# Multi-query attention with residual on one Trainium2 core: two instruction paddings in the front in place of nine, and the last four residuals loaded earlier in the final list

## The chip, the cores and the metric

The kernel runs on one core of a Trainium2 chip. The metric is the device time of one launch in microseconds (us); a lower one is better. TensorE is called PE (its weight loads PEld), VectorE DVE, ScalarE ACT, GpSimd POOL and SyncE SP. Every DMA that this text speaks of is issued by SP, in the order of the program.

## The reference

Sixty-four batches of 128 tokens with 512 features go through a layer norm, multi-query attention with 16 heads of width 64 (one key and value head for all), an output projection, a second layer norm, and a residual sum. All is float32.

```
xn  = layernorm(x, g_in)                              # 64 x 128 x 512
q   = (xn @ Wq).reshape(b, n, 16, 64) * 64 ** -0.5
kv  = xn @ Wkv                                        # one head: k, v
k, v = null_kv and kv, concatenated along the tokens  # 129 keys
sim = einsum('bhid,bjd->bhij', q, k) + bias           # bias per head, null column
sim = where(causal or mask, -max, sim)
out = einsum('bhij,bjd->bhid', softmax(sim), v) @ Wo
y   = x + layernorm(out, g_out)
```

## The kernel before

**Tiling.** Tokens come in groups of four batches (512 tokens, 16 groups). Two batches are one round of the main loop, `cycle(c)` for c from 1 to 29. A round does several things for different batches side by side: it loads and norms the tokens of a later group, makes the queries of the next group (`q_one`, seven products in the manner of Strassen's scheme per pair of feature tiles), the exponentials and sums of its own two batches (`exps`, `rinv`, `scale`), the output projection of the two batches before (`out_one`), the output norm and the store of the two before those, and, in `region(c)`, the scores of the next two batches and the product of the present ones with the values. Queries of group 0 are made in a plain way by `q_half(c, h)`: four matrix products of 128 x 128 by 128 x 256 into one PSUM tile, 8 pairs of a weight load and a matmul in the instruction stream, and then a copy by ACT. The PSUM tile of `q_half(c, 1)` has one of two buffers, X for even c and Y for odd c, so it waits for the copy of `q_half(c - 2, 1)`.

**Order.** Nothing reorders the program (`tc.manual_schedule()`): each engine works through its instructions in the order in which the Python code makes them. The code has a front written out by hand (L1079 to L1229: group 0, first scores, first queries of group 1), the loop (L1230), and a final list written out by hand (L1234 to L1375) for the last six batches, in which the output norm is cut into `pair_stats`, `pair_pow`, `pair_center`, `pair_scale` and `store`.

**Paddings.** `nc.tensor.addr_align(256, offset=k)` fills PE's instruction stream with NOPs until the next instruction stands k slots behind a multiple of 256 slots. A weight load, a matmul, a NOP and a wait on a semaphore of its own are one slot each. There are nine such calls in the front (L1151, L1156, L1161, L1167, L1177, L1188, L1200, L1213, L1218) and one in each round of the loop (L1058), with the offset 223, or 183 in the last round, ahead of `region(c)`.

**Residuals and stores.** `load_res(b)` (L131) takes a buffer of 128 x 512 and loads the input x[b] again; `pair_scale(b)` (L822) adds it to the normed output on DVE; `store(b)` (L835) writes the result. Residuals take the two `res` buffers, those of the last four batches the three `x` buffers, which held input tokens in the loop. The outputs y of a round are in three buffers called `y`; those of the last six batches are in one tile of their own, `y_end`. A load into a buffer waits for the last reader of what the buffer held, and SP, which issues it, waits with all that stands behind. In the final list the order on SP is: load_res(B-6), load_res(B-5), store(B-8), load_res(B-2), load_res(B-4), load_res(B-3), load_res(B-1), store(B-7), store(B-6), store(B-5), store(B-3), store(B-4), store(B-2), store(B-1), with B = 64. Ahead of it stand the stores and the two residual loads of round 29.

## Time and profile before

| | us |
|---|---|
| median of 3 runs | 1051.45 (1051.0 to 1051.99) |
| the profiled execution, its own time | 1052.77 |
| its span, from the first to the last instruction | 1051.0 |
| PE busy | 1028.5 |
| DVE busy | 772.0 |
| POOL busy | 710.1 |
| ACT busy | 665.5 |
| mean granted TensorE clock | 0.994 |

The span is what the profile's views divide; the time of the execution has 1.77 us more, which lie before and after the instructions. The three runs were taken without the profiler. A row of a timeline gives start, length, engine, line, operation, tiles and count, and in brackets the idle time ahead of it and what ended it. "issue" in that place means that the profile shows no wait. A row of the windows gives, for one stretch, its length, the busy time of PE, PEld, DVE, ACT and POOL, the granted clock of TensorE, the busy share of the 16 DMA engines and the GB/s that they moved.

### The profile page before, as it was taken

How to read it: one execution, taken by the hardware profiler on the slowest of the kernel's cores; microseconds unless marked ns; L12 is line 12 of the kernel's file. 1: busy time of each engine (PE TensorE's matmuls, PEld its weight loads, DVE VectorE, ACT ScalarE, POOL GpSimd, SP SyncE). 2: the span in 40 equal slices, each digit the busy share in tenths (PEclk: the TensorE clock that was granted, in tenths of full speed). 3: DMA queues.
4: the chain of work that ended last, by engine and by line, in shares of the span. 5: the costliest groups of instructions: out<-in, count | busy, mean ns of one | idle time of the engine just before them, and what ended most of it. 6: DMA issues, size and time to landing. Idle time of an engine off the chain costs nothing.

```text
span 1051.0 us, 31264 instructions
## 1 busy us (share of the span) xinstructions
PE 1028.5 (98%) x11856; PEld 899.5 (86%) x11856; DVE 772.0 (73%) x1664; ACT 665.5 (63%) x2799; POOL 710.1 (68%) x530
## 2 busy tenths in 40 slices
PE   9699999999999999999999999999999999999996
PEld 8588888888888888888888888888888888888875
DVE  7467777776868767877776867767877776766698
ACT  3267766667766667766667766667765667755581
POOL 3478767577575776767577575776767577676774
PEclk9899999999999999999999999999999999999999
DMA  6615052341514315052341514316052341502103
GB/s 213 153 50 140 22 159 77 110 131 47 157 50 133 113 62 171 25 160 77 111 131 46 158 48 133 113 66 170 26 152 80 109 131 47 159 7 82 42 7 135
DMA packets 68690, 105.12 MB, mean 100 GB/s; under 512 B 8640, under 2 KB 32832, under 8 KB 66752
## 3 DMA queue, kind: packets, MB, share of 16 engines
q1 hardware_dynamic: 67440, 102.08, 32.0%
q8 instruction: 97, 1.59, 0.7%
q10 hardware_dynamic: 1104, 1.05, 0.3%
q14 instruction: 49, 0.40, 0.1%
HBM read 67.45 MB, written 35.65 MB: 98 GB/s over the span
## 4 chain that ended last, share of the span: by engine, by line
PE 77%; DVE 8%; ACT 6%; POOL 4%; DMA 2%; issue 2%; SPq 0%; POOLq 0%; ACTq 0%; DVEq 0%
PE pa L493 16%; PE pyX L755 15%; PE pyY L755 8%; PE pc L493 8%; PE ps L548 8%; PE pkv L355 5%; PE pyw L755 4%; PE pw L493 4%; PE poX L665 4%; ACT s L596 3%; PE pq L442 3%; DMA xT<-xd 2%; PE pos L665 2%; POOL s L617 1%; DVE sb L632 1%
## 5 line engine op out<-in xcount | busy, mean ns | idle before, releaser
L596 ACT ACTIVATE s<-s,nmax 128x65 f32<-128x65 f32 (+1 forms) x1024 | 377.3, 392 | 0.0
L532 POOL TENSOR_TENSOR s<-biasp,mneg 128x1552 f32<-128x1552 f32 x64 | 206.2, 3223 | 70.7 <-DVE sb L632 58.9
L617 POOL TENSOR_TENSOR s<-s,rinv 128x1024 f32<-128x1024 f32 (+1 forms) x128 | 190.0, 1485 | 56.9 <-DVE rinv L613 56.9
L596 ACT ACTIVATION_READ_ACCUMULATOR s<-s,nmax 128x1 f32 x1024 | 220.2, 215 | 0.0
L632 DVE STREAM_TRANSPOSE sb<-s 128x1536 f32<-128x1536 f32 x64 | 113.5, 1773 | 42.4 <-POOL s L617 42.2
L582 DVE TENSOR_TENSOR s<-ps,s 128x256 f32<-128x256 f32 (+2 forms) x224 | 120.1, 607 | 18.0 <-PE ps L548 15.7
L493 PE MATMUL pa<-xS,wq 128*128 128x256 f32 x480 | 123.4, 379 | 0.5 <-ACT ku L504 0.5
L755 PE MATMUL pyX<-wo,oT 128*128 128x256 f32 x512 | 121.6, 380 | 0.2 <-POOL oT L738 0.2
L738 POOL TENSOR_TENSOR yS<-oT 128x512 f32<-128x512 f32 x32 | 40.7, 1273 | 118.3 <-ACT oT L705 114.2
L705 ACT ACTIVATE oT<-poX,nv 128x256 f32<-128x256 f32 x59 | 28.0, 474 | 143.8 <-PE poX L665 74.4
L587 DVE TENSOR_REDUCE nmax<-s 128x8 f32<-128x520 f32 (+1 forms) x128 | 116.6, 951 | 0.0
L755 PE MATMUL pyX<-wT,oT 128*128 128x256 f32 x488 | 115.4, 379 | 0.3 <-POOL oT L738 0.3
L755 PEld LDWEIGHTS pyX<-wo,oT 128*128 128x128 f32 x512 | 96.8, 190 | 15.3 <-issue 1.3
L755 PEld LDWEIGHTS pyX<-wT,oT 128*128 128x128 f32 x488 | 92.6, 190 | 13.3 <-POOL oT L738 0.7
L493 PEld LDWEIGHTS pa<-xS,wq 128*128 128x128 f32 x480 | 88.9, 190 | 11.7 <-ACT ku L504 0.9
L548 PEld LDWEIGHTS ps<-kT,qT 64*64 64x64 f32 x4096 | 85.6, 134 | 11.3 <-issue 11.1
L548 PE MATMUL ps<-kT,qT 64*64 64x128 f32 (+1 forms) x4096 | 93.7, 245 | 0.3 <-issue 0.3
L514 DVE TENSOR_TENSOR qT<-pc,ku 128x256 f32<-128x256 f32 x120 | 50.4, 420 | 58.4 <-ACT ku L504 43.1
L511 ACT COPY qT<-pa 128x256 f32<-128x256 f32 x60 | 23.0, 383 | 101.9 <-PE pa L493 101.9
L665 PE MATMUL pos<-sb,vr 32*64 32x128 f32 (+1 forms) x1792 | 81.0, 321 | 0.0
L285 POOL TENSOR_TENSOR rstd<-rstd,nhalf 128x1 f32<-128x1 f32 x64 | 35.6, 558 | 66.0 <-DVE rstd L284 66.0
L665 PE MATMUL poY<-sb,vr 32*64 32x128 f32 x720 | 74.4, 347 | 0.0
(113 smaller groups left out, 2306.1 us busy)
## 6 DMA issues: line engine op xcount, KB each, us to landing
x<-in_x_dram SPq DMA_DIRECT2D x64, 256.0 KB, 5.1
res<-in_x_dram SPq DMA_DIRECT2D x64, 256.0 KB, 3.0
out_dram<-y SPq DMA_DIRECT2D x58, 256.0 KB, 2.0
xd<-xb SPq DMA_DIRECT2D x14, 1024.0 KB
xT<-xd SPq DMA_DIRECT2D x56, 256.0 KB, 6.2
vr<-vd SPq DMA_DIRECT2D x64, 128.0 KB, 8.6
kT<-kd SPq DMA_DIRECT2D x64, 64.0 KB, 9.6
kd<-kb SPq DMA_DIRECT2D x16, 128.0 KB
```

Of the source, the lines that this page charges most:

```text
L355: nc.tensor.matmul(pkv, xT[g][:, t, kc, :], wkv[:, kc, :], start=(kc == 0), stop=(kc == KC - 1),)
L493: nc.tensor.matmul(prod[tag], w[:, kc, f * P : (f + 1) * P], t[:, :, kc, :], start=(start and kc == 0), stop=(kc == HK - 1), skip_group_ch ...
L514: nc.vector.tensor_tensor(o, p, k, ALU.add)
L532: nc.gpsimd.tensor_tensor(S[b], biasp, mneg[:, t].unsqueeze(1).broadcast_to([P, R8, ROW]), ALU.add,)
L548: nc.tensor.matmul(to[r][i * DH : (i + 1) * DH, f, :], qT[g][rows, f, t, NQ - 1 - i if hf else i], kT[g][rows, 0 : NQ if hf else NQ // 2, ...
L582: nc.vector.tensor_tensor(sv, ps, sv, ALU.add)
L587: nc.vector.tensor_reduce(nmax[b][:, hf], S[b][:, :, WITH_NULL[hf]], AX.X, ALU.max, negate=True)
L596: nc.scalar.activation(row, row, AF.Exp, bias=nmax[b][:, hf, k : k + 1], accum_out=rsum[b][:, hf, k : k + 1],)
L617: nc.gpsimd.tensor_tensor(sv, sv, rinvs.pop((b, hf)).unsqueeze(2).broadcast_to([P, R8, sv.shape[2]]), ALU.mult,)
L632: nc.vector.transpose(sb.rearrange("p j e q -> p e j q"), S[b][:, :, 1 : ROW - 1].rearrange("p e (j k) -> p e j k", k=Q),)
L665: nc.tensor.matmul(po[s][rows, half], vr[g][quad(s), j, t, :], sb[quad(s), slots, r * NF : (r + 1) * NF, :], start=start, stop=True, skip_ ...
L755: nc.tensor.matmul(prod[key], h[:, c, :], w[:, c, :], start=(start and c == 0), stop=(c == HC - 1), skip_group_check=not start,)
```

## The change

Seven of the nine paddings in the front go; the other two, at L1161 and L1188, get other offsets (244 for 149, 86 for 24). The paddings of the loop stay. In the final list, the residual loads of the last four batches move to its head, in the order B-4, B-3, B-2, B-1; the one of batch B-1 takes a `y` buffer, since three `x` buffers hold the others. No other instruction moves; each store of the final list now has no residual load between it and the store before, save load_res(B-6) and load_res(B-5), which stay.

```
     def load_res(b):
-        pool, tag = (xp, "x") if b >= B - 4 else (rp, "res")
-        res[b] = pool.tile([P, DIM], FP, tag=tag, name=f"res_{b}")
+        if b == B - 1:
+            res[b] = hp.tile([P, DIM], FP, tag="y", name=f"res_{b}", bufs=3)
+        else:
+            pool, tag = (xp, "x") if b >= B - 4 else (rp, "res")
+            res[b] = pool.tile([P, DIM], FP, tag=tag, name=f"res_{b}")
         nc.sync.dma_start(out=res[b], in_=x[b])
...
-    nc.tensor.addr_align(256, offset=79)
     q_half(5, 1)
     exps(0, 0, 0, 4)
     scores_max(1, 0)
     scores_max(1, 1)
-    nc.tensor.addr_align(256, offset=114)
     q_half(6, 1)
     exps(0, 0, 4)
     rinv(0, 0)
     scale(0, 0)
-    nc.tensor.addr_align(256, offset=149)
+    nc.tensor.addr_align(256, offset=244)
     q_half(7, 1)
     exps(0, 1, 0, 2)
     q_one(0, 1, 0)
     weight_sum(3)
     exps(0, 1, 2, 4)
-    nc.tensor.addr_align(256, offset=192)
     q_one(0, 2, 0)
...
-    nc.tensor.addr_align(256, offset=236)
     q_half(0, 1)
...
-    nc.tensor.addr_align(256, offset=24)
+    nc.tensor.addr_align(256, offset=86)
     q_half(1, 1)
...
-    nc.tensor.addr_align(256, offset=92)
     q_one(0, 1, 1)
...
-    nc.tensor.addr_align(256, offset=143)
     q_half(2, 1)
...
-    nc.tensor.addr_align(256, offset=186)
     q_half(3, 1)
...
+    load_res(B - 4)
+    load_res(B - 3)
+    load_res(B - 2)
+    load_res(B - 1)
     values_out(B - 6, (1, 3))
     values_out(B - 6, (0, 2))
...
     pair_stats(B - 5)
-    load_res(B - 2)
-    load_res(B - 4)
     out_one(B - 4, 6)
-    load_res(B - 3)
     out_one(B - 4, 3)
...
     pair_center(B - 7)
-    load_res(B - 1)
     out_one(B - 4, 7)
```

More of the change, by code (lines that the diff above doesn't have):

```diff
@@ L131, in load_res @@
     def load_res(b):
-        pool, tag = (xp, "x") if b >= B - 4 else (rp, "res")
-        res[b] = pool.tile([P, DIM], FP, tag=tag, name=f"res_{b}")
+        if b == B - 1:
+            res[b] = hp.tile([P, DIM], FP, tag="y", name=f"res_{b}", bufs=3)
+        else:
+            pool, tag = (xp, "x") if b >= B - 4 else (rp, "res")
+            res[b] = pool.tile([P, DIM], FP, tag=tag, name=f"res_{b}")
         nc.sync.dma_start(out=res[b], in_=x[b])
@@ L1150 @@
         token_sum(1, k)
-    nc.tensor.addr_align(256, offset=79)
     q_half(5, 1)
@@ L1155 @@
     scores_max(1, 1)
-    nc.tensor.addr_align(256, offset=114)
     q_half(6, 1)
@@ L1160 @@
     scale(0, 0)
-    nc.tensor.addr_align(256, offset=149)
+    nc.tensor.addr_align(256, offset=244)
     q_half(7, 1)
@@ L1166 @@
     exps(0, 1, 2, 4)
-    nc.tensor.addr_align(256, offset=192)
     q_one(0, 2, 0)
@@ L1176 @@
     norm_stats(9)
-    nc.tensor.addr_align(256, offset=236)
     q_half(0, 1)
@@ L1187 @@
     scale(1, 0)
-    nc.tensor.addr_align(256, offset=24)
+    nc.tensor.addr_align(256, offset=86)
     q_half(1, 1)
@@ L1199 @@
     norm_apply(8)
-    nc.tensor.addr_align(256, offset=92)
     q_one(0, 1, 1)
@@ L1212 @@
     norm_apply(10)
-    nc.tensor.addr_align(256, offset=143)
     q_half(2, 1)
@@ L1217 @@
     tokens_T(10)
-    nc.tensor.addr_align(256, offset=186)
     q_half(3, 1)
@@ L1232 @@
     at_end.append(gp.tile([P, 8, DIM], FP, tag="qT", name="y_end"))
+    load_res(B - 4)
+    load_res(B - 3)
+    load_res(B - 2)
+    load_res(B - 1)
     values_out(B - 6, (1, 3))
@@ L1314 @@
     pair_stats(B - 5)
-    load_res(B - 2)
-    load_res(B - 4)
     out_one(B - 4, 6)
-    load_res(B - 3)
     out_one(B - 4, 3)
@@ L1329 @@
     pair_center(B - 7)
-    load_res(B - 1)
     out_one(B - 4, 7)
```

## The prediction

> **What bounds the kernel now.** I read the page first: its busy times, the slices, and the chain of work that ended last.

> ```profile
> span 1051.0 us, 31264 instructions
> PE 1028.5 (98%) x11856; PEld 899.5 (86%) x11856; DVE 772.0 (73%) x1664; ACT 665.5 (63%) x2799; POOL 710.1 (68%) x530
> PEclk9899999999999999999999999999999999999999
> ...
> PE 77%; DVE 8%; ACT 6%; POOL 4%; DMA 2%; issue 2%; SPq 0%; POOLq 0%; ACTq 0%; DVEq 0%
> ```

> TensorE (PE) is busy 98% of the span and carries 77% of the chain, so a microsecond taken from its queue early on is a microsecond off the end, unless the tail or another engine takes it back. The second slice of PEclk (26 to 53 us) is the only one at 8. So I asked next what the weight loads (PEld, the first half of each matmul pair) wait for: us in total, times, the longest.

> ```profile
> PEld pq L442 <- issue: 10.0, 3, 9.3
> ```

> Of three waits of L442, which is `q_half`, one is 9.3 us long. The reader is to look for a single long gap of the bounding engine rather than for its busy share. The timeline of the weight loads places it, and the answers for the lines of the paddings say what PE's sequencer did then (columns: min/median/max ns, first and last start):

> ```profile
> 34.56 1.59 PEld L442 LDWEIGHTS pq<-xT,wq 128*128 128x128 f32 x8 [0.17 <-issue]
> 45.43 7.87 PEld L442 LDWEIGHTS pq<-xT,wq 128*128 128x128 f32 x24 [9.28 <-issue]
> 53.32 0.84 PEld L493 LDWEIGHTS pa<-xT,wq 128*128 128x128 f32 x4
> ...
> 56.78 1.70 PEld L442 LDWEIGHTS pq<-xT,wq 128*128 128x128 f32 x8
> 58.50 0.84 PEld L493 LDWEIGHTS pa<-xS,wq 128*128 128x128 f32 x4
> ```

> ```profile
> L1151 PEldq NOP  x152: 13/13/13, 34.0 to 45.4; - x152
> L1156 PEldq NOP  x19: 13/13/13, 45.5 to 46.8; - x19
> L1218 PEldq NOP  x19: 13/13/13, 68.6 to 69.9; - x19
> L1058 PEldq NOP  x30: 13/13/13, 101.8 to 104.0; - x30
> ```

> A padding is a run of NOPs that PE's sequencer executes one by one: 152 of them in 11.4 us, 0.075 us each. The first padding, L1151, holds 152; the other eight of the front hold 19 each (first and last of eight such rows are shown); that of round 1 of the loop, at L1058, holds 30. While the NOPs run, PE works off what was queued ahead of them (34.0 to 36.15, some 2.1 us), and then stands still until 45.43. The windows give the second price of that stop, the granted clock (the number behind the POOL column):

> ```profile
> 45.00:51.00 6.00, 5.54 (x13) 4.49 (x14) 0.00 (x0) 1.71 (x9) 0.00 (x0) 0.50 0.93 217
> ```

> After the stop PE runs at half clock: 0.50 from 45 to 51 us.

> **The change part by part: how many NOPs are left.** Between two paddings lie (difference of the offsets, mod 256, less the NOPs of the second) slots of real instructions. Before L1151 the stream stands at 79 - 152 = 183 mod 256. To L1161 come (114-79-19) + (149-114-19) = 32 slots, so without the first two paddings it stands at 215, and the new target 244 takes **29** NOPs. To L1188 come 24 + 25 + 25 = 74 slots: 318, that is 62, and the target 86 takes **24**. To L1218 come 49 + 32 + 24 = 105: 191 in place of 186. Round 1 has 223 - 186 - 30 = 7 mod 256 slots up to its own padding, so it stands at 198 and takes **25** in place of 30. From there every round stands on 223 as before, so the main loop keeps its slots, and its paddings cost what they cost. The front goes from 152 + 8 x 19 + 30 = 334 NOPs to 78: exactly 256 fewer.

> **The first padding.** Without it q_half(5,1) follows q_half(4,1) at 34.56 + 1.59 = 36.15. Eight pairs at full clock take 58.50 - 56.78 = 1.72 us, so the 24 pairs of three `q_half` take 5.16, and q_one(0,1,0) starts at 41.3 in place of 53.32: **12.0 us** (9.28 of standing still, and 7.89 - 5.16 = 2.73 of half clock). [...]

> What could be late next is ACT, DVE or POOL, which had the stop to catch up in:

> ```profile
> 36.59 0.37 ACT L449 COPY qT<-pq 128x256 f32<-128x256 f32 x1 [6.01 <-PE pq L442]
> 49.25 0.37 ACT L449 COPY qT<-pq 128x256 f32<-128x256 f32 x1 [12.29 <-PE pq L442]
> 49.52 0.35 ACT L596 ACTIVATE s<-s,nmax 128x65 f32<-128x65 f32 x1
> ```

> ```profile
> 36.32 1.83 DVE L587 TENSOR_REDUCE nmax<-s 128x8 f32<-128x520 f32 x2
> 39.92 1.82 DVE L587 TENSOR_REDUCE nmax<-s 128x8 f32<-128x520 f32 x2
> ...
> 41.28 1.26 POOL L475 TENSOR_TENSOR xS<-xT,xS 128x512 f32<-128x512 f32 x1
> ```

> ACT idled 12.29 us for PE. Afterwards it has the copies of q_half 5, 6 and 7 and, in between, eight exponentials of 0.35 to do: copy at 38.1, four exponentials to 39.9, copy at 39.9, four to 41.7, copy of q_half(7,1) at 41.7, 0.4 after PE begins q_one. It stood at the same distance before. Their maxima are ready at 38.15 (36.32 + 1.83), the second batch's at 41.74, and POOL's token sums at 42.5, ahead of q_one(0,5,0) at 43. So nobody is later than PE by more than before, and I count the 12.0 whole.

> **The other paddings of the front.** Removing 19 NOPs that lie beside queued matmuls gives nothing, except at L1213, where PE had little queued:

> ```profile
> 68.25 1.59 PEld L442 LDWEIGHTS pq<-xT,wq 128*128 128x128 f32 x8 [0.59 <-issue]
> ```

> ```profile
> 104.81 1.27 PEld L755 LDWEIGHTS pyX<-wT,oT 128*128 128x128 f32 x6
> ```

> That gap goes: 0.5, bounds 0 and 0.6. The new 29 at L1161 take 29 x 0.073 = 2.1 us of the sequencer (19 take 1.3 in the L1156 row). I assume that it comes to them once the wait of q_half(6,1) for the first copy above ends, 36.96; they end at 39.1, and PE has work queued to 36.15 + 2 x 1.72 = 39.6. I take 0; the bound is 2.1 if none is covered. The 24 at L1188 are five more than now, 0.36 us, of which I take 0.1, bounds 0 and 0.36. The 25 of round 1 are fewer than the 30 that leave no gap now (the second row, the first work behind them, has no idle time in brackets). Sum of the front: 12.0 + 0.5 - 0.1 = **12.4**.

> **The tail.** SyncE's queue (SPq) is worked off in order. Its rows at the end, and the last norm:

> ```profile
> 976.44 4.75 SPq L836 DMA_DIRECT2D out_dram<-y  x2
> 981.24 50.08 SPq L134 DMA_DIRECT2D res<-in_x_dram  x4
> 1031.36 0.42 SPq L836 DMA_DIRECT2D out_dram<-y  x1
> 1031.84 8.48 SPq L134 DMA_DIRECT2D res<-in_x_dram  x4
> 1040.37 0.43 SPq L836 DMA_DIRECT2D out_dram<-y  x1
> 1040.84 7.52 SPq L836 DMA_DIRECT2D out_dram<-y_end  x6
> ```

> ```profile
> 1047.25 0.75 DVE L824 SCALAR_TENSOR_TENSOR y_end<-y_end,rstdo,res 128x512 f32<-128x512 f32 x1 [0.44 <-POOL rstdo L799]
> ```

> Four loads, one DMA of 256 KB and some 0.43 us of SPq each, move from behind store(B-8) (1031.84 to 1040.3, the last one waiting for a buffer) to right after the pair at 981; they pass load_res(B-6), load_res(B-5) and store(B-8). Three go into `x` buffers that are long free. load_res(B-1) now waits for a `y` buffer, so for the landing of the store that ends its issue at 981.2; behind it stands load_res(B-6), which waits for the norm of batch B-8 near 1022 anyway, so nobody waits for it. In return store(B-7) goes out some 9 us earlier, and those of B-6, B-5 and B-3 right behind their norms. But the end hangs on the last: its norm ends at 1047.25 + 0.75 = 1048.0, the store is issued at once (1040.84 + 7.52 = 1048.36), and that norm waits for POOL, not for a DMA. The queue is already empty when B-2 and B-1 come. I cost the tail at **0**; bounds 0.9 either way, two more or two fewer issues of 0.43 ahead of the last.

> **The sum.** The profiled execution has a span of 1051.0 (1052.77 with what lies around it): 1051.0 - 12.4 = 1038.6. The median of the runs shown is 1051.45, so 1051.45 - 12.4 = **1039.0**. A measurement of this kernel tells about 0.2%, 2.1 us, from no change.

> **The rivals.**

> (a) *The data come too late for the shorter front.* The loads for the third group of tokens are issued at 34 to 36, ahead of the 2 MB of `wo`:

> ```profile
> L127 SPq DMA_DIRECT2D x<-in_x_dram x4: 532/602/741, 34.0 to 36.0; - x4
> L280 DVE BATCH_NORM_STATS2 st<-x x4: 643/683/684, 58.1 to 64.6; 128x6 f32<-128x512 f32 x4
> 40.00:50.00 10.00, 4.54 (x11) 3.67 (x12) 1.74 (x3) 0.75 (x4) 2.54 (x3) 0.55 1.03 243
> ...
> 56.00:58.00 2.00, 2.00 (x11) 1.77 (x10) 0.01 (x1) 1.85 (x9) 0.00 (x0) 1.00 0.04 9
> 67.88 0.21 DVE L293 TENSOR_SCALAR nmr<-mv,rstd 128x1 f32<-128x1 f32 x1 [1.79 <-POOL rstd L285]
> ```

> Their statistics move from 58.1 to 64.6 to 46.1 to 52.6. The DMA engines are full to 50 and empty by 57. If the last tile landed only at 57, DVE would wait 4.4 us; 1.79 of that is idle a little later, so 2.6 could reach PE: 1041.6. Against it: those 1 MB were issued first, and 243 GB/s from 40 on move them in about 4 us, were they served first. Chance 0.11.

> (b) *The 29 NOPs are not covered*, because the sequencer reaches them later: up to 2.1 us more, 1041.1. Chance 0.03.

> [...] Chance 0.03, and 0.02 for a stop ending near the point itself, which would be no change.

> (d) *The change doesn't do what it says:* my count of slots is off by 30 or more, so that the stream is past 244 and the padding wraps. Up to 255 NOPs are 19 us, less 2.1 covered, plus 2.7: 1051.45 + 19.6 - 12.4 = 1058.7. The counts come out of nine offsets and their NOPs without remainder, so 0.01.

> **How the numbers follow.** The forecast alone has 0.80. Low: 0.2 more at L1188 and L1213, 0.9 of the tail and 0.5 of run to run (1051.0 to 1051.99): 1039.0 - 1.6 = 1037.4. High: the 2.1 of (b), 0.26 and 0.5 of the small paddings, 0.9 of the tail and 0.5 between runs: 1039.0 + 4.3 = 1043.3, which takes in (a). Faster 0.94, the same 0.02, slower 0.04.

> **What would show it.** Right: no gap of L442 above 0.6 us, a granted clock of 1.00 from 34 to 55, NOP rows of 29, 24 and 25, region(0) (the first L548 after 54 us) at 63 in place of 75.39, rounds as long as before, and the last norm and its store at the same distance from it. Wrong: a new wait of DVE at L280 (a), a gap before L442 near 40 (b, c), NOP rows near 255 (d), or another distance from the last loop round to the end, in the tail.

## The result, and the profile after

The changed kernel takes **1040.22 us** (median of 4 runs, 1039.57 to 1040.68) against 1051.22 of the kernel before, timed beside it (1050.59 to 1051.99): 11.0 us less, a ratio of 0.9895 with a 95% interval of 0.9877 to 0.9912. Forecast were 1039.0 in a range of 1037.4 to 1043.3. Line numbers differ a little from those of before: `q_half` is L445, `q_one` L496, the scores L551, the values L668, the paddings L1061, L1162 and L1187. e3_before and e5_split below have the line numbers of before.

The page of the kernel after, the same lines as before: span, busy times, clock, instruction fetches, chain.

```profile
span 1038.8 us, 31012 instructions
PE 1024.2 (99%) x11856; PEld 896.4 (86%) x11856; DVE 771.2 (74%) x1664; ACT 665.9 (64%) x2799; POOL 711.0 (68%) x530
PEclk9999999999999999999999999999999999999999
...
q8 instruction: 96, 1.57, 0.7%
...
PE 92%; ACT 3%; DVE 3%; DMA 1%; POOL 1%; issue 1%; POOLq 0%; DVEq 0%; ACTq 0%
```

The profiled execution took 1040.6 us, its span is 12.2 shorter than that of before. PE's own work is smaller by only 4.3 (1028.5 to 1024.2); the rest of the gain was idle time. The 8 in the second slice of PEclk is gone, PE's stream is 256 NOPs shorter (29 + 24 + 25 for 334 up to round 1), there is one instruction fetch less, and PE carries 92% of the chain in place of 77%. The row of the fetches in the page of before (packets, MB, share of the DMA engines' time):

```profile
q8 instruction: 97, 1.59, 0.7%
```

The timeline of PE's weight loads in the front of after:

```profile
32.95 2.18 PEld L551 LDWEIGHTS ps<-kT,qT 64*64 64x64 f32 x108
35.30 6.77 PEld L445 LDWEIGHTS pq<-xT,wq 128*128 128x128 f32 x32 [0.17 <-issue]
42.09 0.84 PEld L496 LDWEIGHTS pa<-xT,wq 128*128 128x128 f32 x4
```

All 32 weight loads of the four `q_half` run in one row of 6.77 us, where before had 8, a stop of 9.28, and then 24 at half clock. From the start of q_half(4,1) to that of q_one(0,1,0) pass 42.09 - 35.30 = 6.79 us, before 53.32 - 34.56 = 18.76. The difference is 11.97. The window from 45 to 51 us and the rows of the three paddings say the rest:

```profile
45.00:51.00 6.00, 6.00 (x29) 5.01 (x28) 3.35 (x9) 4.93 (x27) 3.26 (x4) 1.00 1.01 233
```

```profile
L1162 PEldq NOP  x29: 13/13/13, 37.8 to 39.9; - x29
L1187 PEldq NOP  x24: 13/13/13, 46.5 to 48.1; - x24
L1061 PEldq NOP  x25: 13/13/13, 90.4 to 92.2; - x25
```

The granted clock is 1.00 where it was 0.50, the NOPs are 29, 24 and 25, as counted, and no gap stands ahead of the first `q_half` or `q_one` behind them. The end of the front in after, and the rows of DVE that explain the gap in it:

```profile
59.49 1.27 PEld L445 LDWEIGHTS pq<-xT,wq 128*128 128x128 f32 x6
61.17 0.73 PEld L496 LDWEIGHTS pc<-xT,wS 128*128 128x128 f32 x4 [0.42 <-DVE qT L517]
...
63.99 0.74 PEld L551 LDWEIGHTS ps<-kT,qT 64*64 64x64 f32 x26 [0.33 <-issue]
```

```profile
57.63 1.29 DVE L330 STREAM_TRANSPOSE xb<-x 128x512 f32<-128x512 f32 x2
59.03 1.78 DVE L635 STREAM_TRANSPOSE sb<-s 128x1536 f32<-128x1536 f32 x1
60.73 0.39 DVE L517 TENSOR_TENSOR qT<-pc,ku 128x256 f32<-128x256 f32 x1
```

The gap of 0.59 at the old L1213 is gone, but PE now waits 0.42 for DVE: the sum L517, of which PE needs the freed buffer, stands behind the transpose L635, which ends at 60.8. region(0) begins at 63.99. From q_one(0,1,0) to there pass 21.90 us, before 75.39 - 53.32 = 22.07: 0.17 gained. In all the front is 11.97 + 0.17 = 12.14 shorter.

The tail of after, SyncE's queue and the last norm:

```profile
963.93 4.74 SPq L839 DMA_DIRECT2D out_dram<-y  x2
968.72 50.39 SPq L137 DMA_DIRECT2D res<-in_x_dram  x8
1019.16 0.90 SPq L839 DMA_DIRECT2D out_dram<-y  x2
1024.82 11.37 SPq L839 DMA_DIRECT2D out_dram<-y_end  x6
```

```profile
1035.07 0.75 DVE L827 SCALAR_TENSOR_TENSOR y_end<-y_end,rstdo,res 128x512 f32<-128x512 f32 x1 [0.44 <-POOL rstdo L802]
```

The loads and stores did move: all eight residual loads are one row, both `y` stores one, and the queue stands empty between 1020.06 and 1024.82. But the last norm still waits 0.44 for POOL, and ends at 1035.82; the last store's issue ends at 1036.19, 2.6 ahead of the end, as before (1051.0 - 1048.36 = 2.6).

### The profile page after: what moved, and what is told of

It is laid out like the page before. It is cut to its first block, busy times and chain, and to the rows that moved or that the text cites. A ratio compares the mean times of both kernels' runs of the same rounds, so it can differ in the third digit from the quotient of the medians.

```text
span 1038.8 us, 31012 instructions
## 1 busy us (share of the span) xinstructions
PE 1024.2 (99%) x11856; PEld 896.4 (86%) x11856; DVE 771.2 (74%) x1664; ACT 665.9 (64%) x2799; POOL 711.0 (68%) x530
## 4 chain that ended last, share of the span: by engine, by line
PE 92%; ACT 3%; DVE 3%; DMA 1%; POOL 1%; issue 1%; POOLq 0%; DVEq 0%; ACTq 0%
PE pa L496 20%; PE pyX L758 19%; PE pc L496 10%; PE pyY L758 9%; PE ps L551 9%; PE pkv L358 5%; PE pyw L758 5%; PE pw L496 5%; PE poX L668 4%; PE pq L445 2%; ACT s L599 2%; PE pos L668 2%; PE poY L668 1%; DMA x<-in_x_dram 1%; DVE y_end L821 1%
## 5 line engine op out<-in xcount | busy, mean ns | idle before, releaser
L635 DVE STREAM_TRANSPOSE sb<-s 128x1536 f32<-128x1536 f32 x64 | 113.5, 1773 | 43.2 <-POOL s L620 43.0
L496 PE MATMUL pa<-xS,wq 128*128 128x256 f32 x480 | 123.4, 379 | 0.5 <-ACT ku L507 0.5
L496 PEld LDWEIGHTS pa<-xS,wq 128*128 128x128 f32 x480 | 88.9, 190 | 11.7 <-ACT ku L507 0.9
L551 PEld LDWEIGHTS ps<-kT,qT 64*64 64x64 f32 x4096 | 85.6, 134 | 11.5 <-issue 11.4
L551 PE MATMUL ps<-kT,qT 64*64 64x128 f32 (+1 forms) x4096 | 93.7, 245 | 0.6 <-issue 0.6
L517 DVE TENSOR_TENSOR qT<-pc,ku 128x256 f32<-128x256 f32 x120 | 50.4, 420 | 58.6 <-ACT ku L507 43.5
L668 PE MATMUL pos<-sb,vr 32*64 32x128 f32 (+1 forms) x1792 | 81.0, 321 | 0.0
L668 PE MATMUL poY<-sb,vr 32*64 32x128 f32 x720 | 74.4, 347 | 0.0
```

The source lines that it names most:

```text
L496: nc.tensor.matmul(prod[tag], w[:, kc, f * P : (f + 1) * P], t[:, :, kc, :], start=(start and kc == 0), stop=(kc == HK - 1), skip_group_ch ...
L517: nc.vector.tensor_tensor(o, p, k, ALU.add)
L551: nc.tensor.matmul(to[r][i * DH : (i + 1) * DH, f, :], qT[g][rows, f, t, NQ - 1 - i if hf else i], kT[g][rows, 0 : NQ if hf else NQ // 2, ...
L635: nc.vector.transpose(sb.rearrange("p j e q -> p e j q"), S[b][:, :, 1 : ROW - 1].rearrange("p e (j k) -> p e j k", k=Q),)
L668: nc.tensor.matmul(po[s][rows, half], vr[g][quad(s), j, t, :], sb[quad(s), slots, r * NF : (r + 1) * NF, :], start=start, stop=True, skip_ ...
```

## The experiments

The kernels ran in three groups, each timed beside the kernel before, whose medians there were 1051.91, 1052.25 and 1052.06 us. Each ratio is to the kernel before of its group. Diffs are against the kernel after, where nothing else is said.

**e1_front and e8_front: the paddings alone**, in two groups. The residual loads have their places and buffers of before.

```diff
...
-    load_res(B - 4)
-    load_res(B - 3)
-    load_res(B - 2)
-    load_res(B - 1)
     values_out(B - 6, (1, 3))
...
+    load_res(B - 2)
+    load_res(B - 4)
     out_one(B - 4, 6)
...
```

> The paddings alone; the final list and its loads stand as before. Theory (the gain is the first padding's stop and its half clock): all of the gain, 1040.2 us, within 0.9 of the changed kernel, and the timeline of PE as in the changed kernel up to the final list. Rival (the earlier loads and stores of the final list carry a part): 1041 or more, by as much as the tail carries.

> The paddings alone once more, five rounds on the same chip as the changed kernel, to put a bound on the loads of the final list. Theory (the tail is worth nothing): within 0.5 us of the changed kernel. Rival (the earlier loads carry some of the gain): above it by 0.5 to 1.

Measured: 1041.36 us, ratio 0.9900 [0.9885, 0.9915], and 1040.72, ratio 0.9893 [0.9877, 0.9910]. 1041.36 is 0.26 outside the 0.9 of the first expectation, but the kernel before was slower in that group, too (1051.91 against 1051.22), and the ratio is that of after (0.9895) within its interval. e8_front isn't above the changed kernel beside it (e7_after, 1041.2), as its rival had it. From q_half(4,1) to region(0) the two take 28.71 and 28.70 us, after 28.69. The whole gain is there without the tail's edit.

**e2_tail: the residual loads alone.** The front has the nine paddings of before, the first of which is shown.

```diff
+    nc.tensor.addr_align(256, offset=79)
     q_half(5, 1)
...
```

> The four residual loads alone; the nine paddings stand as before. Theory (the last store hangs on the last norm, which waits for no load): 1051.2 us, within 0.9. Rival: 1050 or less, and a shorter way from the last loop round to the end.

Measured: 1052.29 us against 1051.91 of the kernel before beside it, ratio 1.0004 [0.9995, 1.0013]: no difference within 1 us. The rows of its tail show the same order on SyncE as in after, and the same wait ahead of the last norm:

```profile
980.17 50.68 SPq L137 DMA_DIRECT2D res<-in_x_dram  x8
1030.90 0.90 SPq L839 DMA_DIRECT2D out_dram<-y  x2
1036.55 11.37 SPq L839 DMA_DIRECT2D out_dram<-y_end  x6
```

```profile
1046.81 0.75 DVE L827 SCALAR_TENSOR_TENSOR y_end<-y_end,rstdo,res 128x512 f32<-128x512 f32 x1 [0.44 <-POOL rstdo L802]
```

**e3_before and e7_after: both kernels once more**, unchanged, to see how far a single profile carries.

> The kernel before, unchanged, to see what in it differs from run to run: its profiled execution lay 12.2 us above that of the changed kernel, but its median only 11.0. Theory (the half clock behind the stop starts and ends where a window that runs by itself has it, so its length differs): the stop of 9.3 us in every profile, but a mean granted clock that differs between runs, 0.994 to 0.997, and with it the time, by 1 to 2 us. Rival (the DMA waits at the start and in the loop differ): the same clock of 0.994 in every run and a spread that stands elsewhere.

> The changed kernel itself, beside its front alone on one chip. Theory: ratio to before 0.989 (a gain of 11.6: 9.2 of stop, 2.3 of half clock in the mean of three profiles of before, 0.1 of the other paddings). Rival (the gain forecast, 12.4, was only masked by a first profile): 0.9882.

Measured: e3_before 1051.91 us, ratio 1.0001 [0.9992, 1.0010]; e7_after 1041.2, ratio 0.9896 [0.9880, 0.9912]. The stop is nearly the same in the second profile of before, but the half clock behind it is shorter. The weight loads of `q_half`, and the window from 45 to 51 us, in e3_before:

```profile
45.33 7.30 PEld L442 LDWEIGHTS pq<-xT,wq 128*128 128x128 f32 x24 [9.23 <-issue]
```

```profile
45.00:51.00 6.00, 5.63 (x16) 4.64 (x17) 0.00 (x0) 1.71 (x9) 0.00 (x0) 0.59 0.91 206
```

The 24 weight loads take 7.30 us instead of 7.87, and the mean clock of the window is 0.59 instead of 0.50. In e2_tail, whose front is that of before, it is 0.57. From the first of the 24 to q_one(0,1,0) pass 7.89 (before), 7.33 (e3_before) and 7.08 us (e2_tail); less the 5.16 of full clock the half clock cost 2.73, 2.17 and 1.92. In all three traces the clock is at half for the same 10.24 us, from 40.94, 39.70 and 39.91 on, while PE resumes at 45.43, 45.33 and 46.06: how much of the 10.24 falls on work differs from trace to trace. That is one cause of the spread between executions, and not shown to be the only one: the mean clocks of the 11 executions of e3_before are 0.992 to 0.995, and their times, 1050.78 to 1053.29 us, don't sort by them. Nor does the ratio of e7_after tell its theory from its rival, as the interval holds both 0.989 and 0.9882; the fronts of the three profiles do, which are 11.6 us longer than that of after in the mean.

**e5_split: the stop in two halves.** The diff is against the kernel before.

```diff
-    nc.tensor.addr_align(256, offset=79)
+    nc.tensor.addr_align(256, offset=3)
     q_half(5, 1)
...
-    nc.tensor.addr_align(256, offset=114)
+    nc.tensor.addr_align(256, offset=38)
     q_half(6, 1)
```

> The kernel before with the 152 NOPs of its first padding halved: 76 stay there and 76 go to the third one (95 in place of 19); all other slots as before. The sequencer then works off its NOPs by 48.3 us either way (34.03 + 76 x 0.075, then 19 + 95 x 0.073). Theory (a stop of 2 to 4 us drops the clock as well, as the one of 2.7 us did without the front's paddings): a first stop of 3.6 us, a clock of 0.50 for one or two times 3.4 us, queued pairs that last twice as long and so cover more NOPs, and q_one at 51.8 in place of 52.7 to 53.3: 1050.4 to 1051. Rival (only a stop of 4.8 us or more, as in the profile of before, drops it): clock 1.00, q_one at 50.0, 1048.6.

Measured: 1050.64 us, ratio 0.9985 [0.9975, 0.9996]. The timeline of `q_half` in e5_split, and the granted clock behind the POOL column of its windows:

```profile
40.72 5.01 PEld L442 LDWEIGHTS pq<-xT,wq 128*128 128x128 f32 x16 [3.48 <-issue]
49.28 3.01 PEld L442 LDWEIGHTS pq<-xT,wq 128*128 128x128 f32 x8 [3.56 <-issue]
```

```profile
42.00:45.00 3.00, 3.00 (x9) 2.34 (x8) 0.83 (x1) 1.64 (x9) 1.65 (x2) 0.50 1.05 265
45.00:48.00 3.00, 1.13 (x5) 0.60 (x3) 0.10 (x1) 1.78 (x10) 0.00 (x0) 0.94 1.05 244
49.00:52.00 3.00, 2.69 (x6) 2.19 (x7) 0.00 (x0) 0.00 (x0) 0.24 (x1) 0.50 0.72 180
```

152 NOPs moved apart still cost two stops, 7.04 us together instead of 9.28, because work is queued ahead of each. In this execution each stop also takes the clock down, for 3.41 us. Not in every one: one such drop is worth 0.0016 of the mean clock, and six of the ten executions have a mean of 0.997 where the traced one has 0.995, so they had one drop at most (at the very end of the span the clock is at half for 3.0 us or more in all 14 profiles, which leaves no room for two). Those six took 1048.74 to 1050.75 us, the other four 1051.29 to 1053.02. The gain is 1.6 us, the interval 0.4 to 2.6. So the price of a padding is its stop (7.04 and 9.28 us here) and, as a term of its own that can be there or not, the clock that it takes with it.

**e4_nofront: the front without any padding.**

```diff
-    nc.tensor.addr_align(256, offset=244)
-    nc.tensor.addr_align(256, offset=86)
```

The 53 NOPs then come to round 1 of the loop, whose padding grows from 25 to 78.

> The changed kernel without its last two paddings in the front, so that round 1 of the loop takes all 78 NOPs in one. Theory (a padding costs what its NOPs last beyond the work queued ahead of them, some 2.1 us): 78 x 0.073 = 5.7, so a stop of about 3.6 us in round 1, too short for the clock to drop, and 1043.8 us. Rival (the queue ahead of PE holds more where the pairs are long, so most is covered): 1042 or less. Second rival (a stop of 3.6 us drops the clock as well): 1045.5.

Measured: 1044.61 us, ratio 0.9932 [0.9919, 0.9946], 3.25 more than e1_front beside it. The round's padding, the weight loads behind it, and the windows:

```profile
L1061 PEldq NOP  x78: 13/13/13, 90.6 to 96.2; - x78
```

```profile
92.69 0.84 PEld L496 LDWEIGHTS pa<-xS,wq 128*128 128x128 f32 x4
96.25 1.71 PEld L758 LDWEIGHTS pyX<-wT,oT 128*128 128x128 f32 x8 [2.71 <-issue]
98.61 3.50 PEld L551 LDWEIGHTS ps<-kT,qT 64*64 64x64 f32 x116 [0.65 <-issue]
```

```profile
98.00:101.00 3.00, 3.00 (x58) 2.39 (x60) 0.34 (x1) 0.37 (x1) 2.78 (x3) 0.50 0.08 33
```

Of 78 NOPs (5.6 us) some 2.9 lie beside queued work, 2.71 are a stop, and that stop, too, took the clock to 0.50, for 3.41 us in the trace. So a stop this short can take the clock; that 3.6 us would be too short for it, as the theory has it, was my assumption. It need not: the fastest of the four executions, 1043.78 us, has a mean clock of 0.998, as after has, and with such a drop 0.997 would be the most. What after's two paddings in the front bring is that the 78 NOPs are spread over three places (29, 24 and 25), each short enough to be covered. There is a second cost in this kernel: in region(0) a weight load of the values (L668) waits 0.84 us, for no semaphore, where after has no gap. e6_nopads shows what that is.

```profile
67.53 0.13 PEld L668 LDWEIGHTS poX<-sb,vr 32*64 32x64 f32 x1 [0.84 <-issue]
```

**e6_nopads: no padding at all.** The diff is against e4_nofront.

```diff
-        if soft:
-            nc.tensor.addr_align(256, offset=183 if c == B // 2 - 3 else 223)
```

> The changed kernel without any padding, in the front or in the loop, so that a multiple of 256 slots falls 26 slots later in each round and passes all its parts. Theory (the paddings of the loop cost nothing, and where a block of instructions begins matters nothing, since no gap of before stands at a block's beginning): as the changed kernel, within 1 us. Rival (they keep the beginnings of blocks at places where a late fetch is covered): in some rounds gaps of PE that no row of the changed kernel has, at the multiples of 256, and a slower time by what they sum up to, 2 us or more.

Measured: 1056.1 us, ratio 1.0026 [1.0012, 1.0040], 15 more than e7_after beside it. Of what PE's weight loads wait for (total, times, longest), the groups of the values L668 in after and then in e6_nopads:

```profile
PEld poX L668 <- issue: 5.2, 30, 0.2
```

```profile
PEld poX L668 <- issue: 8.8, 37, 0.9
PEld pos L668 <- issue: 6.0, 10, 1.0
...
PEld poY L668 <- issue: 1.8, 3, 0.9
```

One such gap in the timeline of e6_nopads:

```profile
165.42 0.24 PEld L668 LDWEIGHTS poX<-sb,vr 32*64 32x64 f32 x2
166.51 0.13 PEld L668 LDWEIGHTS poX<-sb,vr 32*64 32x64 f32 x1 [0.85 <-issue]
```

It waits for nothing that the profile shows. But if the slots of the stream are counted from the trace's rows (weight loads, matmuls, NOPs and waits), every gap over 0.25 us of this kind lies at a multiple of 256 exactly: slot 5.00 x 256 (0.44 us), 8.00 (0.55), 11.00 (0.61), 14.00 (0.86), 17.00 (0.96), and so on in steps of 3 x 256 slots, some 20 of them. The 19 in the values sum up to 11.4 us, most of the 15. Ahead of each, by 2.2 to 3.2 us, the trace has the packet of an instruction fetch. From round to round the place moves through the values, as a round without its 26 NOPs has 742 slots, and the rounds in which it lies outside them have no such gap, except two with a smaller one right behind the values (0.53 and 0.32 us). So the paddings of the loop are worth their place, and the rival by which a late block of instructions stops PE is real, only not ahead of region(0).

**e10_off173, e11_off203, e12_off233: the same number of NOPs in the loop, at another place.** If a late block is the cause, it must come back in every round when the padding sends the multiple of 256 to a bad place. The diff is that of e11_off203; e12_off233 has 193 and 233 there, and e10_off173, which also lacks the two paddings of the front, 133 and 173.

```diff
-            nc.tensor.addr_align(256, offset=183 if c == B // 2 - 3 else 223)
+            nc.tensor.addr_align(256, offset=163 if c == B // 2 - 3 else 203)
```

> After without its two front paddings and with the offsets of the loop's padding 50 lower (173, and 133 in the last round); round 1 has about 28 NOPs, every later round the same 26 as after. Theory A (a block of 256 slots is asked for when PE's sequencer enters the one before it, and takes some 3.6 to 4.2 us to arrive; the small matmuls of region work off 256 slots in 3.3 us, so a block that begins and ends inside them is late): the multiples of 256 now fall at pair 41 of the scores and pair 41 of the values, a gap of 0.3 to 0.9 us at that pair of the values in every round, none waiting for a semaphore, 29 x 0.5 = some 14 us more than after, 1055 (1050 to 1062). Rival B (what the loop's paddings bring is that every round has the same place, or the time that their NOPs give the transfers; which place does not matter): as after, 1041.

> After with the offsets of the loop's padding 20 lower (203, and 163 in the last round), the front as in after; round 1 has 5 NOPs, every later round the same 26. The multiples of 256 fall at pair 26 of the scores and pair 26 of the values. Theory A: the request for the second of these blocks comes when the sequencer, which runs some 18 pairs ahead, passes pair 26 of the scores, now some 8 pairs after region's start instead of before it, so the gap at the values is there, smaller than with 173 or equal: 0.2 to 0.8 us in every round, 1047 to 1062. Rival B: as after, 1041.

> After with the offsets of the loop's padding 10 higher (233, and 193 in the last round), the front as in after; round 1 has 35 NOPs, every later round the same 26. The multiples of 256 fall at pair 11 of the scores and of the values, so the request still comes before region's start. Theory A: no gap in the values, as after, 1041 to 1042 (the 35 NOPs of round 1 cost at most 0.7 us). Rival B: as after, too. A third reading, that 223 alone fits: slower by some us.

Measured, on one chip: e10_off173 1051.45 us, ratio 0.9997 [0.9987, 1.0006]; e11_off203 1041.18, ratio 0.9894 [0.9879, 0.9908]; e12_off233 1039.94, ratio 0.9884 [0.9867, 0.9900]. A shift of 30 slots against e11_off203 costs 10 us, nearly the whole gain of the change. The missing paddings of the front aren't the reason: from q_half(4,1) to region(0) e10_off173 takes 28.69 us, as after. The gap in round 7 of e10_off173:

```profile
254.98 2.67 PEld L551 LDWEIGHTS ps<-kT,qT 64*64 64x64 f32 x128 [0.33 <-issue]
257.82 0.13 PEld L668 LDWEIGHTS poX<-sb,vr 32*64 32x64 f32 x2 [0.17 <-issue]
...
258.20 0.13 PEld L668 LDWEIGHTS poX<-sb,vr 32*64 32x64 f32 x1
259.03 0.13 PEld L668 LDWEIGHTS poX<-sb,vr 32*64 32x64 f32 x2 [0.70 <-issue]
```

and its wait of the values, beside that of e12_off233:

```profile
PEld poX L668 <- issue: 12.1, 48, 0.7
```

```profile
PEld poX L668 <- issue: 5.2, 30, 0.2
```

In 25 of the 28 rounds from region(1) to region(28) of e10_off173 a gap of up to 0.70 us stands at the same place, 33 or 34 pairs into the values; together 7.4 of the 10.0 us by which the way from the start of region(1) to that of region(29) is longer (890.16 us; 880.13 in after). Most of the rest, 2.5 us, stands ahead of the keys' product (L358), for which the profile shows no releaser. Theory A is thus right in that the place of the multiple alone brings a late block in nearly every round, and rival B falls. When a block is asked for, and that it arrives 3.6 to 4.2 us later, was my estimate and is not shown; the traces show when its packet starts. I had the place wrong, and with it what e11_off203 would give: I had counted from the padding, but 8 pairs of `out_one` stand between it and the first score, so the multiple falls at pair 33 of the scores here, 18 in e11_off203, 8 in after and 3 in e12_off233. What decides is seen in the fetches. The packet nearest to the first score of a region comes 1.5 us ahead of it in after and in e12_off233 (median of 28 rounds), 0.44 ahead in e11_off203, and 1.16 behind it in e10_off173. The scores are 128 pairs, exactly 256 slots, worked off in 2.84 us (254.98 to 257.82 above), and in the late cases the first instruction of the next block runs 2.3 to 3.0 us behind the packet. So in these four runs the block whose packet starts 1.16 us behind the first of the small pairs comes late, and those whose packets start 0.44 to 1.5 us ahead of it don't. What the expectation had too large is the size: 0.30 us per gap on average instead of 0.5.

That the stream comes in blocks of 256 slots is read from the traces: after has 24716 slots and 96 packets of 16.4 KB, one for some 257 slots, and in e6_nopads the gaps lie at multiples of 256. What the fetches cost is hidden in the rounds of after, and is some 10 us in e10_off173.

**e9_swap: the new wait of DVE taken out of the front.**

```diff
-    blocks_T(1)
-    bias_add(3)
     norm_apply(10)
     q_half(2, 1)
     norm_apply(11)
     q_one(0, 7, 1)
+    blocks_T(1)
+    bias_add(3)
```

> After with one thing moved: the transposes and bias additions blocks_T(1), bias_add(3) of the front stand behind q_one(0,7,1) instead of ahead of q_half(2,1), so that DVE's copy of the token sums for the next product is no longer behind them. Theory (the 0.42 us gap of PE at pair 424 is this wait of DVE): the gap goes, the front from pair 304 to pair 440 is 0.3 to 0.4 us shorter (28.3 against 28.7), the time 1040.7, not to be told from after by its median. Rival (something else of the front is late behind it): the gap moves to another line, no change of the span of the front.

Measured: 1040.7 us, ratio 0.9889 [0.9874, 0.9904]; its weight loads show the gap gone:

```profile
58.75 1.70 PEld L445 LDWEIGHTS pq<-xT,wq 128*128 128x128 f32 x8
60.47 0.84 PEld L496 LDWEIGHTS pc<-xT,wS 128*128 128x128 f32 x4
```

The front, from q_half(4,1) to region(0), takes 28.41 us instead of 28.69: 0.3 less, seen in the profile and not in the medians. That settles what took back most of the gain at L1213. Neither e9_swap nor e12_off233 can be told from after by its time.

## Why the prediction was right, point by point

**The first padding: right in mechanism and size for its own profile.** Forecast 12.0, measured 11.97 between the two profiles that were compared. The mis-sized part is the half clock in it: 2.73 was the most expensive of three profiles, whose mean is 2.27. From q_half(4,1) to region(0) e3_before takes 40.18 and e2_tail 39.94 us, where the profile of before has 75.39 - 34.56 = 40.83 and that of after 63.99 - 35.30 = 28.69; against those two the front is shorter by 11.5 and 11.25 us, not by 12.1. This term should have had a bound on the low side.

**L1213: half a miss.** With L1188 the prediction counted 0.5 - 0.1 = 0.4; the stretch behind q_one(0,1,0) gained 0.17. The step said that nobody is later than PE by more than before. That was worked out for ACT's copies and the maxima, and holds there; 20 us further on it failed, where DVE's sum stands behind the transpose L635. e9_swap shows that wait and its 0.3 us.

**The new paddings: right.** 29, 24 and 25 NOPs, no gap behind them. e4_nofront shows how near the bound was: 78 in one place are 2.71 us of stop.

**The tail: right.** Forecast 0, measured 1.0004 [0.9995, 1.0013]. The wait for POOL ahead of the last norm is unchanged at 0.44, so nothing that SyncE does earlier can reach the end.

**Rival (a)** did not come: the statistics of the third group run from 46.88 to 53.34 in after, forecast 46.1 to 52.6, and that execution was 0.74 later (35.30 for 34.56) before the first padding already. **Rival (c)**, a block of instructions that comes late (chance 0.03, and 0.02 for no change), did not come in the front: no gap stands ahead of L445 near 40, and e4_nofront and e10_off173, without any padding in the front, have none there either, up to region(0). How many blocks are held ahead, on which this rival depends, no run shows. The loop's own late blocks (e6_nopads, e10_off173) suggest why it didn't come: near 40 us the front consists of large pairs, 0.21 us each (6.77 us for 32), of which 256 slots are worked off in some 27 us, so that a fetch has time even when the DMA engines are full. The trace of after shows it: the multiple of 256 that lies 12 slots behind the new padding is passed at 41.66 us and the next one at 64.16, and between them one fetch packet starts, as late as 49.52, with the DMA engines full up to 50 (a share of 1.04 to 1.09 in the four windows of 2 us from 42 on), and takes 1.34. It comes some 13 us early all the same. I gave the rival its chance from that fullness; here the rate at which the slots are worked off decided. **Rivals (b) and (d)** are out by the rows of the NOPs.

**The sum.** Forecast 12.4, measured 11.0 by the medians, and 11.25 to 12.1 by the three profiles of the front. The half clock's size (0.5 on the mean) and L1213 (0.2) account for 0.7 of the 1.4. The other 0.7 isn't settled: the loop differs by as much from run to run (its rounds exceed 31.45 us by 0.8 to 1.7 in all in three profiles with the old front, and by 0.55 to 1.9 in five with the new one), among others at gaps of up to 1.0 us ahead of the keys' product, for which these profiles show no releaser.

## What to carry to other kernels

In these runs a padding cost nothing while the engine had work queued ahead of its sequencer (2.1 to 2.9 us, some 30 to 40 NOPs), and beyond that its stop (2.71 us for 78 NOPs, 9.28 for 152) and, where the stop took the clock down, the work done at half clock (1.92 to 2.73 us in the three profiles with 152); so split a long one over places that are each covered, or let it go. What a padding is worth is another question than what it costs: find the multiples of 256 slots in the trace, and ask whether a whole block lies among small, fast instructions (here 128 pairs in 2.84 us, with 2.3 to 3.0 us from a packet's start to the first instruction of its block). And a term that differs from profile to profile, as the half clock does here (2.73, 2.17 and 1.92 us), is to be sized from several, not from one.

## What the runs showed of the hardware

**A whole block of small instructions outran its fetch in e6_nopads and e10_off173.** In the region 256 slots are worked off in 2.84 us, in the late cases the fetched block's first instruction ran 2.2 to 3.2 us behind the start of the fetch's packet, and the loss was up to 0.96 us a time. Two such places are left in the profile of after, in the last region and the scores behind it, at multiples 92 and 93 of 256: gaps of 0.41 and 0.74 us, which no run here tried to take away.
